# Order at the joints of an attention and clustering kernel: fillers dealt out anew, the last MLP sums by channel half, a fifth value pair ahead of the first score

## The chip, the cores and the metric

The kernel runs on one core of one Trainium2 chip. All data is float32. The metric is the device time in microseconds of one execution; the time before is the median of three.

TensorE multiplies matrices and writes to PSUM. VectorE (DVE in the profile), ScalarE (ACT) and GpSimd (POOL) do the rest, each through its own queue in the order in which the program issues its instructions. SyncE (SP) starts most transfers.

## The reference

The input x is 4 images of 256 channels by 64 x 64 positions. Two layers follow each other; N is 4096 positions of an image.

```python
# layer 0: attention over all positions
q = einsum('oc,bcn->bno', wq, xf) + bq          # 32 channels
k = einsum('oc,bcn->bon', wk, xf) + bk
attn = softmax(einsum('bnd,bdm->bnm', q, k), axis=-1)
v = einsum('oc,bcn->bon', wv, xf) + bv          # 256 channels
x = gamma * einsum('bcn,bmn->bcm', v, attn) + x
# layer 1: clustering, MLP, pointwise convolution
y = x + ls1 * cluster(group_norm(x, gn1_w, gn1_b), ...)
hdn = conv1x1(gelu(conv1x1(group_norm(y, gn2_w, gn2_b), w1)), w2)
y = y + ls2 * hdn
z = relu(batch_norm(y * dw_w))
z = relu(batch_norm(conv1x1(z, pw_w)))
```

`group_norm` takes one mean and one variance over a whole image. `cluster` makes features and values (96 channels each, 4 heads), cuts the image into 2 x 2 folds, pools 4 centres in each, gives every point to the centre that is most alike, sums the values of each centre's points, divides by their count, hands the result back to the points and projects it to 256 channels.

## The kernel before, in words

The images go through one after the other. In each there are three stages: attention, clustering, MLP. The order of all instructions is written by hand (`tc.manual_schedule()`), and so is the work of the next image that is slipped into the gaps of this one.

**Attention.** The positions are cut in 8 blocks of 512 queries, and 8 groups of 512 keys, so there are 64 units. `score` multiplies the keys of a group with the queries of a block (sc, L333), four 32-row products side by side. `exps` subtracts the column maximum, which has been spread over the partitions (mb, L383), and takes the exponential. `weigh` multiplies with the values (av, L408). Scores run ahead of the weighting by some units. For image 0 there is nothing to hide the beginning behind, and `alone` does it: keys (kp, L262), four blocks of queries (qp, L304), copies of the queries by DMA (q), value pairs (`v_pair`, two halves vp, L285, with one ScalarE copy, L293), and then the first 8 scores with a value pair behind each. Their maxima are folded (`fold`, L363), transposed (tt, L369) and reduced (L371), made a diagonal (dg, L373) and spread by a product (mb).

**Clustering.** `cluster` is a chain of many short steps on VectorE, ScalarE and TensorE. To keep TensorE busy in it there are *fillers*: a list of closures, from which each call `fill(n)` takes the next n. In images 0, 1 and 2 it is the list `projections` of the next image, 35 items:

```python
parts.projections = [lambda i=i: v_half(i) for i in range(N // P)]
parts.projections[26:26] = [lambda: k_half(0), lambda: q_four(0), lambda: k_half(1)]
```

so items 0 to 25 are value halves, 26 to 28 are the two key halves and the queries, and 29 to 34 the last six value halves. In image 3 the list comes from `late_block`: the last block of image 2's MLP, 16 matmuls `first`, 16 `second` (mol, L1005), an empty item and 4 `last` (pwl, L1028). The n of all calls add up to 35; what is left when the MLP begins is done there at once (`fill(N)`).

At the clustering's end stand, in the order of the program: a first sum over pooling weights (agg, L820), `similar(1)` and, after it, `fill(3)`; `largest(1)` and `weights(1)` on VectorE (to L760 and L763); the counts (cnt, L841), which need L760; the second sum; transposes; the projected centres gp with `fill(1)` behind; and then the hand-back in two rounds of four quarters and two channel halves (op, L911):

```python
products(0, 0, range(4))
products(0, 1, (0, 1))
seen(0, 0)
fill(2)
products(0, 1, (2, 3))
fill(2)
products(1, 0, range(4))
...
fill(5)
```

Channel half 0 is added to x by VectorE (L923), half 1 by ScalarE (L935) and GpSimd (L936). `seen` takes the statistics for the second group norm (`bn_stats`, L895). `group_norm` aggregates them (L214), averages over the partitions with two tiny matmuls (gnm, L216 and L217), has a filler, a third tiny matmul (gnv, L226), the root on ScalarE, and again fillers; then it loads the Gelu table, and the scale and shift are ready (L234, L235).

**MLP.** GpSimd makes three sums of weights (L1059 to L1061). Then come 8 blocks of 512 positions (7 in image 2), 4 steps each. `first` makes two hidden tiles from seven half-size products (hp, hu, hq, L1126), with sums on VectorE (L1162), and Gelu on ScalarE (L1155). `second` is a generator of four matmuls (mo, L1133) that add two hidden tiles i to two channel halves c; it is taken piece by piece between the products of the next step. For the last step of the last block two pieces are taken before the next image's maxima are transposed and two after. `finish` adds the sums to y (L1206) and appends the relu (L1196) to the hooks; `last` is the pointwise convolution (pw, L1102), whose output is evicted by ScalarE (L1112) and stored.

Of the kernel before, what the change touches and what calls it, by code (L numbers as in the profile page):

```python
# [13 lines left out]
P = 128  # L14
B, C, H, W = 4, 256, 64, 64
N = H * W
KC = C // P
# [6 lines left out]
HID = 4 * C  # L24
# [4 lines left out]
RG, GRP = 4, N // NB  # L29
# [16 lines left out]
def attention_then_cluster_block(  # L46
# [17 lines left out]
    nc = tc.nc  # L64
# [19 lines left out]
    def loaded(name, ap, shape):  # L84
        t = const.tile(shape, F32, name=name)
        nc.sync.dma_start(out=t, in_=ap)
        return t
# [38 lines left out]
    w2_s = loaded("w2_s", w2.rearrange("(k p) m -> p k m", p=P), [P, HID // P, C])  # L126
    wpw_s = loaded("wpw_s", wpw.rearrange("(k p) m -> p k m", p=P), [P, KC, C])
# [15 lines left out]
    def par(name, k=None):  # L143
        i = PC.index(name)
        return pc_s[:, :, i] if k is None else pc_s[:, k, i : i + 1]

    def pvc(name, p=P, off=0):
        i = PV[name] + off
        return pv_s[:p, i : i + 1]

    def rsqrt(dst, src, eps, meanwhile=lambda: None):

        nc.vector.tensor_scalar(dst, src, eps, None, ALU.add)
        nc.scalar.activation(dst, dst, AF.Sqrt)
        meanwhile()
        nc.vector.reciprocal(dst, dst)
# [49 lines left out]
    def table(f):  # L206

        nc.scalar.activation(probe, probe, f)

    def group_norm(b, which, stats, fill, meanwhile=lambda: None):  # L210

        nm = f"{which}_{b}"
        mv = small.tile([P, 2], F32, tag="mv", name=f"mv_{nm}")
        nc.vector.bn_aggr(mv, stats.rearrange("p i s -> p (i s)"))  # L214
        ps1 = ps_a.tile([P, NB], F32, tag="a0", name=f"gnm_{nm}")
        nc.tensor.matmul(ps1[:, 0:1], left, mv[:, 0:1], start=True, stop=True)  # L216
        nc.tensor.matmul(ps1[:, 1:2], avg, mv[:, 0:1], start=True, stop=True)  # L217
        fill(1)
        dv = small.tile([P, 2], F32, tag="dv", name=f"dv_{nm}")
        nc.vector.tensor_copy(dv, ps1[:, 0:2])  # L220
        nc.vector.scalar_tensor_tensor(
            mv[:, 1:2], dv[:, 0:1], dv[:, 0:1], mv[:, 1:2], ALU.mult, ALU.add
        )
        nc.vector.tensor_scalar(dv[:, 1:2], dv[:, 1:2], -1.0, None, ALU.mult)
        ps2 = ps_a.tile([P, NB], F32, tag="a1", name=f"gnv_{nm}")
        nc.tensor.matmul(ps2[:, 0:1], avg, mv[:, 1:2], start=True, stop=True)  # L226
        rstd = small.tile([P, 1], F32, tag="rstd", name=f"rstd_{nm}")
        rsqrt(rstd, ps2[:, 0:1], GN_EPS, meanwhile)
        fill(3 if which == "gn1" else 1)
        if which == "gn2":  # L230
            table(AF.Gelu_apprx_tanh)
        ga = small.tile([P, KC], F32, tag="ga", name=f"ga_{nm}")
        gb = small.tile([P, KC], F32, tag="gb", name=f"gb_{nm}")
        nc.vector.tensor_scalar(ga, par(f"{which}_w"), rstd, None, ALU.mult)  # L234
        nc.vector.scalar_tensor_tensor(gb, ga, dv[:, 1:2], par(f"{which}_b"), ALU.mult, ALU.add)  # L235
        return ga, gb
# [9 lines left out]
    def attention(b, xs):  # L246
# [7 lines left out]
        def k_half(i):  # L254

            if i == 0:
                own["k"] = big.tile([P, GRP, P], F32, tag="k", name=f"k_{b}")
            ps = ps_m.tile([P, 2, 2, P], F32, tag="m", name=f"kp_{b}_{i}")
            for t in range(2):
                for k in range(KC):  # L260
                    for r in range(RG):
                        nc.tensor.matmul(  # L262
                            ps[r * D : (r + 1) * D, t],
                            wqk_s[:, k, 1],
                            xs[2 * i + t][:, k].rearrange("p (g r n) -> p r g n", g=2, r=RG)[:, r],
                            start=(k == 0),
                            stop=(k == KC - 1),
                        )
            nc.scalar.activation(
                own["k"][:, 4 * i : 4 * i + 4, :].rearrange("p (t g) n -> p t g n", t=2),  # L270
                ps,
                AF.Identity,
                bias=bqk_s[:, 1:2],
            )
# [3 lines left out]
        def v_half(i):  # L278
            if i == 0:
                own["v"] = big.tile([P, N // P, C], F32, tag="v", name=f"v_{b}")  # L280
            if i % 2 == 0:
                vps[0] = ps_m.tile([P, 2, C], F32, tag="m", name=f"vp_{b}_{i // 2}")
            o = (i * P) % XT
            for k in range(KC):
                nc.tensor.matmul(  # L285
                    vps[0][:, i % 2, :],
                    xs[i * P // XT][:, k, o : o + P],
                    wv_s[:, k, :],
                    start=(k == 0),
                    stop=(k == KC - 1),  # L290
                )
            if i % 2:
                nc.scalar.copy(own["v"][:, i - 1 : i + 1, :], vps[0])  # L293

        def v_pair(i):
            v_half(2 * i)
            v_half(2 * i + 1)
# [165 lines left out]
        def alone():  # L463

            nc.vector.tensor_scalar(fb_w, ones[:ED], pvc("f_b", ED), None, ALU.mult)
            k_half(0)
            q_four(0)
            q_block(0, nc.gpsimd)
            q_block(1, nc.gpsimd)
            for i in range(4):  # L470
                v_pair(i)
            for u in range(GRP):
                if u == RG - 1:
                    k_half(1)
                hooks, maxima = [], []
                score(u, hooks, maxima)
                for f in hooks + maxima:
                    f()
                v_pair(u + 4)
            fold(0)  # L480
            for i in range(GRP + 4, GRP + 6):
                v_pair(i)
            half["dg"] = across(0)
            v_pair(GRP + 6)
            spread(0, half["dg"])
            v_pair(GRP + 7)
            exps(0)
            score(GRP)
# [133 lines left out]
    def cluster(b, ys, stats, cells, rest, fill, gelu):  # L622
# [30 lines left out]
        for k in range(KC):  # L653
# [4 lines left out]
                start=(k == 0),  # L658
                stop=(k == KC - 1),
# [118 lines left out]
        for nb in range(NBLK):  # L778
# [7 lines left out]
            ps = ps_s.tile([P, 2, 2, C], F32, tag="s", name=f"fv_{b}_{nb}")  # L786
            for j in range(4):
                g = j // 2
                for k in range(KC):
# [4 lines left out]
                        start=(k == 0),  # L794
                        stop=(k == KC - 1),
# [34 lines left out]
        heads(NBLK - 1)  # L830
        similar(1, lambda: fill(2))
        gelu(1)
        fill(3)
        table(AF.Sqrt)
        largest(1)
        weights(1)
# [3 lines left out]
        for j in range(8):  # L840
# [4 lines left out]
                start=(j == 0),  # L845
                stop=(j == 7),
# [9 lines left out]
        def turned(hb):  # L856
# [27 lines left out]
            start=True,  # L884
            stop=True,
# [64 lines left out]
        seen(0, 1)  # L950
        seen(1, 0)
        seen(1, 1)
        fill(5)
        return stats2


# [94 lines left out]
    def mlp(b, ys, stats2, fill, nxt, blocks):  # L1051
# [42 lines left out]
        def quarters(t):  # L1094
            return t[:, 0, :HB], t[:, 0, HB:], t[:, 1, :HB], t[:, 1, HB:]

        def last(nb):
            zs = pairs.pop(nb)
            ps = ps_s.tile([P, 2, NB], F32, tag="s", name=f"pw_{b}_{nb}")
            for c in range(KC):  # L1100
                for k in range(KC):
                    nc.tensor.matmul(  # L1102
                        ps[:, c, :],
                        wpw_s[:, k, c * P : (c + 1) * P],
                        zs[:, 1, k, :],
                        start=(k == 0),
                        stop=(k == KC - 1),
                    )

            def out_c(c):  # L1110
                o_s = zs[:, 0, c, :]
                nc.scalar.activation(  # L1112
                    o_s, ps[:, c, :], AF.Relu, scale=pw_s[:, c : c + 1], bias=pw_e[:, c : c + 1]
                )
                nc.sync.dma_start(out=ob[:, c, nb * NB : (nb + 1) * NB], in_=o_s)

            for c in range(KC):
                hooks.append(lambda c=c: out_c(c))
# [8 lines left out]

        def second(nb, acc, hs, j):

            for i in range(2):  # L1130
                jj = j + HID // P // 2 * i
                for c in range(KC):
                    yield nc.tensor.matmul(  # L1133
                        acc[c],
                        w2_s[:, jj, c * P : (c + 1) * P],
                        hs[:, i],
                        start=(j == 0 and i == 0),
                        stop=(j == HID // P // 2 - 1 and i == 1),
                    )

        def first(nb, j, todo):

# [71 lines left out]
        def hook():  # L1214
            while hooks:
                hooks.pop(0)()
# [5 lines left out]
        acc, todo = None, iter(())  # L1222
# [5 lines left out]
        for nb in range(blocks):  # L1228
            for j in range(4):
                hs = first(nb, j, todo)  # L1230
                if j == 0:
                    if nb:
                        finish(nb - 1, acc)
                    acc = [
                        ps_a.tile([P, NB], F32, tag=f"a{c}", name=f"mo{c}_{b}_{nb}")
                        for c in range(KC)
                    ]
# [20 lines left out]
        hook()  # L1258
        if nxt:
            nxt.exps(0)  # L1260
        last(blocks - 1)
        hook()
        if blocks < NBLK:
            y = []
# [14 lines left out]
    with tc.manual_schedule():  # L1279
# [3 lines left out]
        for b in range(B):  # L1283
# [10 lines left out]
            fill = filler(todo)  # L1294
# [81 lines left out]
```

## Time and profile before

| | |
|---|---|
| device time, median of 3 | 3477.98 us (3476.77 to 3483.36) |
| profiled span | 3476.0 us |
| TensorE busy | 3421.1 us (98%) |
| VectorE busy | 2046.2 us (59%) |
| ScalarE busy | 1683.9 us (48%) |
| GpSimd busy | 1489.2 us (43%) |
| mean granted TensorE clock | 0.997 of full |

A profile line of the timeline has a start in us from the span's start, a length in us, the engine, the line, the operation, what it writes and reads, the shape and how many instructions were merged; a bracket at the end tells how long the engine was idle before it, and which instruction ended that. Matmuls are pipelined, so the length of a merged line overlaps the next line's start a little, and it is the starts that show the pace. A float32 matmul counts as two instructions.

Image 0 takes from 0 to about 920 us, of which the attention ends at about 590, the clustering at about 670. The later images are laid out in the same way.

### The profile page before, as it was taken

Reading aid. Unit: us, or ns where it says so; the run is one execution under the profiler, and the core shown is the slowest. Engines: PE = TensorE matmul, PEld = TensorE weight load, DVE = VectorE, ACT = ScalarE, POOL = GpSimd, SP = SyncE. Lnnn points to the kernel's source line nnn. Section 1 sums busy time; section 2 is a strip of 40 time slices with the busy share of each in tenths; the row PEclk is TensorE's granted clock in tenths of the full one; section 3 lists DMA queues with packets and bytes.
Section 4 is the critical chain, followed back from the end, with each engine's and each line's share of the span. In section 5 each row is a group of like instructions: output and inputs, shape, how many; then the busy total and the mean of one; then the engine's idle time right before and its main releaser. Section 6 shows DMA issues by size and latency. Waiting matters only on the chain.

```text
span 3476.0 us, 31760 instructions
## 1 busy us (share of the span) xinstructions
PE 3421.1 (98%) x11760; PEld 1694.3 (49%) x11760; DVE 2046.2 (59%) x2912; ACT 1683.9 (48%) x2157; POOL 1489.2 (43%) x799
## 2 busy tenths in 40 slices
PE   8999999999999999999999999999999999999999
PEld 4444445655444444565544444466554444445565
DVE  4666664645566666464556666646446666664543
ACT  5545553444554554344455555434445554544444
POOL 2656665211265665521126566552104665672200
PEclk9999999999999999999999999999999999999999
DMA  2000001000000000100000000000000000000000
GB/s 91 7 4 3 7 0 49 7 19 13 20 5 4 3 7 12 37 7 19 19 16 4 3 5 5 19 30 7 19 19 10 4 7 3 4 0 1 13 19 25
DMA packets 25260, 47.16 MB, mean 14 GB/s; under 512 B 6704, under 2 KB 8592, under 8 KB 25104
## 3 DMA queue, kind: packets, MB, share of 16 engines
q1 hardware_dynamic: 20240, 38.29, 3.2%
q10 hardware_dynamic: 4608, 6.30, 0.8%
q8 instruction: 93, 1.52, 0.2%
q0 software_dynamic: 256, 0.52, 0.1%
q14 instruction: 63, 0.52, 0.0%
HBM read 19.93 MB, written 16.78 MB: 11 GB/s over the span
## 4 chain that ended last, share of the span: by engine, by line
PE 94%; DVE 3%; ACT 1%; DMA 0%; issue 0%; SPq 0%; POOL 0%; ACTq 0%; DVEq 0%
PE av L408 52%; PE mo L1133 12%; PE sc L333 8%; PE hu L1126 4%; PE pw L1102 3%; PE hp L1126 3%; PE hq L1126 3%; PE vp L285 2%; PE fv L790 2%; PE mb L383 1%; PE den L429 1%; PE op L911 1%; PE qp L304 0%; PE kp L262 0%; PE tt L369 0%
## 5 line engine op out<-in xcount | busy, mean ns | idle before, releaser
L408 PE MATMUL av<-s,v 128*128 128x512 f32 x4096 | 1826.5, 597 | 0.6 <-ACT s L398 0.6
L408 PEld LDWEIGHTS av<-s,v 128*128 128x128 f32 x4096 | 758.9, 190 | 1024.6 <-issue 1015.1
L403 POOL TENSOR_TENSOR acc<-acc,s 128x1024 f32<-128x1024 f32 x448 | 1057.5, 2361 | 466.1 <-ACT s L398 446.7
L398 ACT ACTIVATE s<-s 128x1024 f32<-128x1024 f32 x512 | 538.7, 1057 | 462.8 <-DVE s L395 429.4
L395 DVE TENSOR_TENSOR s<-s,mb 128x1024 f32<-128x1024 f32 x512 | 595.2, 1207 | 6.5 <-PE mb L383 6.5
L1133 PE MATMUL mo<-hs,w_s 128*128 128x512 f32 x992 | 508.4, 596 | 3.8 <-ACT hs L1155 1.6
L355 DVE TENSOR_TENSOR top<-sc,top 128x1024 f32<-128x1024 f32 x196 | 239.9, 1224 | 388.0 <-PE sc L333 388.0
L1155 ACT ACTIVATE hs<-hs,pv_s 128x256 f32<-128x256 f32 x496 | 251.3, 508 | 360.9 <-DVE hs L1162 350.1
L351 ACT COPY s<-sc 128x1024 f32<-128x1024 f32 x224 | 226.1, 1009 | 350.9 <-PE sc L333 350.9
L1162 DVE TENSOR_TENSOR hs<-hu,hs 128x256 f32<-128x256 f32 x372 | 157.8, 424 | 355.0 <-ACT hs L1165 205.5
L1088 POOL TENSOR_TENSOR xn<-xn 128x256 f32<-128x256 f32 x27 | 23.8, 881 | 681.7 <-DVE xn L1075 433.4
L333 PE MATMUL sc<-q,k 32*128 32x512 f32 x2048 | 294.0, 640 | 1.4 <-DMA q<-q 1.4
L400 POOL TENSOR_TENSOR acc<-s 128x1024 f32<-128x1024 f32 x32 | 75.1, 2347 | 476.9 <-ACT s L398 476.9
L358 DVE TENSOR_TENSOR top<-sc,top 128x1024 f32<-128x1024 f32 x196 | 240.1, 1225 | 47.5 <-ACT s L351 30.9
L356 ACT COPY s<-sc 128x1024 f32<-128x1024 f32 x224 | 226.9, 1013 | 76.0 <-DVE top L355 39.8
L1162 DVE TENSOR_TENSOR hs<-hq,hs 128x256 f32<-128x256 f32 x372 | 146.4, 421 | 107.5 <-PE hq L1126 103.3
L1133 PEld LDWEIGHTS mo<-hs,w_s 128*128 128x128 f32 x992 | 186.9, 190 | 42.7 <-ACT hs L1165 7.3
L333 PEld LDWEIGHTS sc<-q,k 32*128 32x128 f32 x2048 | 81.0, 182 | 192.5 <-issue 106.6
L1126 PE MATMUL hp<-xn,w_s 128*128 128x256 f32 x496 | 150.6, 385 | 2.7 <-DVE xn L1075 2.7
L1126 PEld LDWEIGHTS hp<-xn,w_s 128*128 128x128 f32 x496 | 92.4, 190 | 73.0 <-issue 62.4
L285 PE MATMUL vp<-wv_s,x 128*128 128x256 f32 x512 | 123.4, 387 | 0.2 <-ACT v L293 0.2
L1102 PE MATMUL pw<-xn,wpw_s 128*128 128x512 f32 x248 | 112.0, 594 | 3.4 <-ACT xn L1196 2.2
(215 smaller groups left out, 2823.0 us busy)
## 6 DMA issues: line engine op xcount, KB each, us to landing
x<-in_x SPq DMA_DIRECT2D x32, 512.0 KB, 4.6
out<-xn SPq DMA_DIRECT2D x62, 256.0 KB, 2.1
q<-q ACTq DMA_DIRECT2D x96, 64.0 KB, 2.0
w_s<-in_w SPq DMA_DIRECT2D x2, 1024.0 KB, 8.9
q<-q SPq DMA_DIRECT2D x24, 64.0 KB, 2.0
q<-q POOLq DMA_DIRECT2D x8, 64.0 KB, 6.4
out<-xl SPq DMA_DIRECT2D x2, 256.0 KB, 2.0
wv_s<-in_wv SPq DMA_DIRECT2D x1, 256.0 KB, 7.1
```

Of the source, the lines that this page charges most:

```text
L333: nc.tensor.matmul(halves[r // 2][:, r % 2, :], k_s[rows, g, :], q_s[rows, :], start=True, stop=True)
L355: nc.vector.tensor_tensor(top, halves[1], top, ALU.max)
L356: nc.scalar.copy(s[:, 2:4, :], halves[1])
L358: nc.vector.tensor_tensor(top, halves[0], top, ALU.max)
L395: nc.vector.tensor_tensor(sh, sh, mxs[nb].unsqueeze(1).to_broadcast([P, 2, NB]), ALU.subtract)
L398: nc.scalar.activation(sh, sh, AF.Exp)
L403: nc.gpsimd.tensor_tensor(acc, acc, s[:, 2 * h : 2 * h + 2], ALU.add)
L408: nc.tensor.matmul(av[c], own["v"][:, RG * g + quarter, c * P : (c + 1) * P], slots[u][:, quarter, :], start=(g == 0 and quarter == 0), st ...
L1126: nc.tensor.matmul(out, w[:, j * P : (j + 1) * P], x, start=True, stop=True)
L1133: yield nc.tensor.matmul(acc[c], w2_s[:, jj, c * P : (c + 1) * P], hs[:, i], start=(j == 0 and i == 0), stop=(j == HID // P // 2 - 1 and i ...
L1155: nc.scalar.activation(dst, src, act, bias=bias)
L1162: nc.vector.tensor_tensor(dst, ps, term, ALU.add)
```

## The change

It moves work and adds none. The fillers are dealt out anew: three more before the counts, four fewer after the last statistics, one more behind gnv in the second group norm. The sum stays 35, and the list's order is the same. It is meant to give TensorE something to do while VectorE works on `largest` and `weights`. The last four mo matmuls of an image's MLP are ordered by channel half, so that the first half's sum is complete after two of them, and the last pw product takes its inputs by k first, so that two of its four matmuls need only the first half's relu. And in image 0 a fifth value pair is put ahead of the first score, which waits for copies of the queries; the pairs behind the scores move up by one.

```diff
@@ group_norm
-        fill(3 if which == "gn1" else 1)
+        fill(3 if which == "gn1" else 2)
@@ alone
-            for i in range(4):
+            for i in range(5):
                 v_pair(i)
             for u in range(GRP):
...
-                v_pair(u + 4)
+                v_pair(u + 5)
             fold(0)
-            for i in range(GRP + 4, GRP + 6):
-                v_pair(i)
+            v_pair(GRP + 5)
             half["dg"] = across(0)
@@ cluster
         gelu(1)
-        fill(3)
+        fill(6)
         table(AF.Sqrt)
...
         seen(1, 1)
-        fill(5)
+        fill(1)
         return stats2
@@ mlp
-        def last(nb):
+        def last(nb, by_k=False):
...
-            for c in range(KC):
-                for k in range(KC):
-                    nc.tensor.matmul(
...
+            for c, k in ((0, 0), (1, 0), (0, 1), (1, 1)) if by_k else ((0, 0), (0, 1), (1, 0), (1, 1)):
+                nc.tensor.matmul(
...
         def second(nb, acc, hs, j):
-            for i in range(2):
+            order = [(i, c) for i in range(2) for c in range(KC)]
+            if nb == blocks - 1 and j == 3:
+                order.sort(key=lambda ic: ic[1])
+            for i, c in order:
                 jj = j + HID // P // 2 * i
...
-        last(blocks - 1)
+        last(blocks - 1, True)
         hook()
```

## The prediction

> **What bounds the kernel now.** I read four views: the page's busy times, TensorE's own waits, the timelines of the clustering's end in images 0 and 3, and the granted clock there. Page first:
>
> ```profile
> PE 3421.1 (98%) x11760; PEld 1694.3 (49%) x11760; DVE 2046.2 (59%) x2912; ACT 1683.9 (48%) x2157; POOL 1489.2 (43%) x799
> ```
>
> TensorE is the bound; no matmul is added or removed, so the time moves only by its idle time (55 us of 3476) and its clock. Its waits (us in total, times, longest) say where the edits can act:
>
> ```profile
> PE cnt L841 <- DVE scr L760: 9.9, 4, 2.7
> ...
> PE gnm_gn L216 <- DVE mv_gn L214: 3.9, 4, 3.2
> ...
> PE pw L1102 <- ACT xn L1196: 2.2, 4, 0.9
> ...
> PE sc L333 <- DMA q<-q: 1.4, 1, 1.4
> ```
>
> The cnt wait is what the three extra fillers are aimed at: 2.7 us in images 0 to 2, 1.7 in image 3. Now what follows it in image 0 (TensorE, then VectorE):
>
> ```profile
> 641.71 1.57 PE L841 MATMUL cnt<-scr,ones 128*96 128x64 f32 x16 [2.71 <-DVE scr L760]
> ...
> 649.27 1.99 PE L285 MATMUL vp<-wv_s,x 128*128 128x256 f32 x8
> ...
> 654.18 1.99 PE L911 MATMUL op<-simt,g 32*128 32x512 f32 x12
> 656.10 1.93 PE L262 MATMUL kp<-x,wqk_s 128*32 128x256 f32 x32
> 657.85 1.90 PE L304 MATMUL qp<-x,wqk_s 128*32 128x512 f32 x16
> ...
> 662.60 3.72 PE L285 MATMUL vp<-wv_s,x 128*128 128x256 f32 x16
> 666.15 0.28 PE L216 MATMUL gnm_gn<-mv_gn,left 128*128 128x1 f32 x2
> ```
>
> ```profile
> 655.36 2.73 DVE L923 SCALAR_TENSOR_TENSOR x<-op,pc_s,x 128x512 f32<-128x512 f32 x4 [1.72 <-PE op L911]
> 658.00 7.20 DVE L895 BATCH_NORM_STATS2 st<-x 128x6 f32<-128x512 f32 x12
> 665.24 0.59 DVE L214 BATCH_NORM_AGGREGATE mv_gn<-st 128x2 f32<-128x96 f32 x1
> ```
>
> From the second round of op (654.18) VectorE works without a pause to the statistics' end, and gnm, which opens the second group norm, comes 0.9 us after L214 began. TensorE has just enough fillers for it: gnm shows no wait. Image 3, whose fillers are shorter, shows the chain's bare length and what it is to lack fillers:
>
> ```profile
> 3213.76 1.99 PE L911 MATMUL op<-simt,g 32*128 32x512 f32 x12
> ...
> 3225.55 0.35 PE L216 MATMUL gnm_gn<-mv_gn,left 128*128 128x1 f32 x2 [3.20 <-DVE mv_gn L214]
> ```
>
> So op to gnm takes VectorE 11.79 us. Last the clock (after the stretch and its length: busy time of PE, PEld, DVE, ACT, POOL, then PEclk, DMA, GB/s):
>
> ```profile
> 3228.00:3229.00 1.00, 1.00 (x3) 0.60 (x3) 0.40 (x3) 0.20 (x1) 1.00 (x2) 0.50 0.00 0
> ...
> 1500.00:1508.00 8.00, 6.96 (x89) 6.41 (x89) 2.55 (x8) 1.02 (x4) 0.00 (x0) 0.57 0.00 0
> 2363.00:2368.00 5.00, 4.76 (x82) 4.50 (x83) 1.60 (x5) 0.04 (x1) 0.00 (x0) 0.66 0.02 3
> 641.00:646.00 5.00, 4.27 (x90) 3.82 (x91) 2.25 (x7) 0.90 (x4) 0.00 (x0) 1.00 0.00 0
> ```
>
> After the cnt wait of images 1 and 2, and the gnm wait of image 3, TensorE ran at half clock for a few us; after image 0's it did not. From cnt to the filler before op takes 4.69 us in image 0, 7.57 in image 1, 6.29 in image 2: half clock cost 2.9 and 1.6 us there.
>
> **What the Trainium skill says.** "TensorE: Matmul & The Clock Gate", What's actually happening: after an idle window of about 3.4 us, free-running, the array drops to half clock, and a busy window brings it back. The trace agrees (0.50 above), but 2.7 us of idle was enough twice in three times. "GPSIMD Engine Reference", Specifications: GpSimd shares SBUF interfaces with VectorE. The trace agrees: L221 takes 1.09 us while GpSimd makes the MLP's weight sums, and 0.22 in the first group norm, where GpSimd is idle. "TensorE: Matmul & The Clock Gate", Architectural detail: ScalarE's queue is strict first-in, first-out; so a table load waits behind a filler's copy (669.42, 0.59 us, then the load, 1.28 us).
>
> **The change part by part.**
>
> *Three fillers before cnt (images 0 to 2).* A half of a value pair takes 0.89 us (20 matmuls in 4.5), three take 2.67 and the wait was 2.71: cnt starts when it did and its idle time is gone. The half-clock spells after it go too; the trace has 4.5 us of them over three images. I take 1.7 us an image, since any phase of a free-running window can be met: of the ways in which a 2.7 us gap can fall on 3.4 us windows about three in four leave one window over half empty, at some 2.2 us each.
>
> *What is handed back.* The list of 35 fillers keeps its order, so all later calls get other items. The two calls between the first op and the second round of op held four value halves (2 times 1.93 us, 3.86). Now they hold a half, the first k half, q and the second k half: 0.93 + 1.8 + 1.83 + 1.8 = 6.36. VectorE had been idle there (1.72), so its chain starts 2.5 us later and gnm comes at 654.18 + 2.5 + 11.8 = 668.5, where it stood at 666.15: 2.3 later. Before gnm TensorE has op (1.92), two halves (1.93), op (1.06) and the lone filler (0.93), 5.84 us, against 11.79: **a new wait of 6.0 us at gnm**. Behind it on TensorE stand two more fillers and the whole MLP.
>
> *After gnm.* The shift of 2.3 shrinks: GpSimd's sums, over at 667.96 now, follow the last op, which comes 0.8 later, so they end by 668.8 and L221 costs 0.2 where it cost 1.09; TensorE's filler now ends last, and gnv comes 1.3 after gnm, where it took 1.88 (minus 0.6). Two fillers after gnv (1.8 us) fill the 0.91 wait of hp, but the Gelu table load stands behind the second one's copy and the first hidden copy 0.15 to 0.2 later than the rest. Net 1.9 to 2.1; I take 1.9.
>
> *Half clock after the new wait.* 6 us of idle fill a window in nearly every phase. The spell then lasts to the end of the first busy window, 3 to 6 us after gnm. Three value halves (2.7 us at full clock) and the MLP's first products lie in it; at spells of 3.4, 4.7 and 6.2 us I lose 1.6, 2.2 and 3.0. I take 2.1.
>
> Per image: 1.9 + 2.1 - 1.7 = +2.3 us; for three, **+7.0**.
>
> *Image 3.* Its fillers are the last block of image 2: 0.86 us matmuls. Three more cost 2.58 against a wait of 1.74, so cnt and all after it come 0.8 later. Matmul (7,0) moves ahead of the last op; its ScalarE relu waits for GpSimd and holds up op's evictions, some 0.3 more. The gnm wait grows from 3.2 to 6. Four pw matmuls follow gnv, where it was three, at half clock in part; the table load stands behind the first one's eviction. **+1.2** (0.3 to 2).
>
> *Fifth value pair before the first score.* Score 0 waits 1.41 us for the fourth q copy (landing at 26.2); a pair takes 1.78. Score 0 ends at 27.27 as now, one pair ahead. Seven pairs later one pair fewer stands between the last score and the transposes: TensorE gets there at 54.1, but fold ends at 54.9, so they start at 54.96 against 55.82. The 0.24 wait of the pair behind goes as well. **-1.1**.
>
> *MLP's last sums by half, pw by k.* In images 0 to 2 finish's first op stands behind dg on VectorE (ends 916.85; the sum was ready by 916.4), so it can't start earlier: 0. At the very end nothing stands before it: half 0's sum is ready 0.86 us sooner, its relu ends at 3465.85 where it was 3466.7, pw starts behind it and the k = 1 matmuls meet the second relu (3467.5) without a wait. The eviction waits for all four matmuls in both orders. **-0.8**.
>
> Sum: 7.0 + 1.2 - 1.1 - 0.8 = +6.3, and with the median of 3477.98 some **3484**.
>
> **The rivals.** (B) *The idle time is really gone*: gnm doesn't wait, the three cnt waits (8.1) and half-clock spells (4.5) are saved, less 0.8 in image 3, plus 1.9 at the ends: 13.7 at most, 3464 to 3470. For it: nothing is added. Against it: 11.79 us of chain and 5.84 us of fillers. (C) *Slower*: the half clock lasts a window longer (another 1.7 us an image) or the MLP's first products, which wait on VectorE five times there already, don't count as busy: 4 images more by 1 to 1.7, 3488 to 3491. For it: image 1's spell after cnt lasted two windows. Against it: image 2's and 3's lasted one.
>
> **How the numbers follow.** The forecast, 3480 to 3487, gets 0.62; C 0.28; B 0.10. The bound of 0.2% is 7 us, 3485: of the forecast 0.47 lies within, 0.15 above. So faster 0.10, within 0.47, slower 0.15 + 0.28 = 0.43. The range 3478.5 to 3490 holds the forecast and most of C and leaves B out.
>
> **What would show it.** Right: cnt without a wait in images 0 to 2; L262 and L304 between the two rounds of op; gnm waiting about 6 us in all four images, half clock after it and none after cnt; the first score's wait gone; pw's wait of 0.9 at the end gone and the three of 0.44 kept. Wrong, if gnm waits under 3 us, or if its L895 group starts at its old distance from cnt.

## The result and the profile after

The change makes the kernel slightly slower: 3489.02 us (median of 6 runs, 3486.53 to 3490.28) against 3479.43 for the kernel before in the same series. The ratio is 1.0027, with a 95% interval of 1.0014 to 1.0040. The profiled spans are 3486.0 and 3476.0 us, so the two traces hold a difference of 10 us as well. In the changed kernel the lines behind the edits have moved by one or two (cnt is L840, op L910, the MLP's products L1124); gnm keeps L216.

The page's busy times of after (engine, us, share of the span, instructions):

```profile
PE 3423.6 (98%) x11760; PEld 1696.6 (49%) x11760; DVE 2042.0 (59%) x2912; ACT 1683.2 (48%) x2157; POOL 1489.9 (43%) x799
```

With the same instructions TensorE is busy 2.5 us longer, at a mean granted clock of 0.994 where it was 0.997, and idle 62.4 us where it was 54.9. TensorE's waits of after (us in total, times, longest) name the idle time:

```profile
PE gnm_gn L216 <- DVE mv_gn L214: 24.0, 7, 6.0
...
PE hu L1124 <- DVE hs L1163: 7.6, 5, 3.8
...
PE pw L1100 <- ACT xn L1197: 1.4, 3, 0.5
...
PE tt L369 <- DVE top L363: 0.8, 1, 0.8
```

The 9.9 us of cnt have left the list, gnm has gone from 3.9 to 24.0, hu from 4.8 to 7.6. Pw keeps its three waits of under 0.5 and has lost the one of 0.9; the first score's 1.4 is now 0.2, and the transposes wait 0.8. TensorE's timeline of after at the end of image 0's clustering (start, length, shape; the bracket is the idle time before):

```profile
640.98 1.57 PE L840 MATMUL cnt<-scr,ones 128*96 128x64 f32 x16
...
646.63 1.99 PE L910 MATMUL op<-simt,g 32*128 32x512 f32 x12
648.55 1.13 PE L285 MATMUL vp<-wv_s,x 128*128 128x256 f32 x4
649.61 1.93 PE L262 MATMUL kp<-x,wqk_s 128*32 128x256 f32 x32
651.48 1.13 PE L910 MATMUL op<-simt,g 32*128 32x512 f32 x4
652.53 1.92 PE L304 MATMUL qp<-x,wqk_s 128*32 128x512 f32 x16
654.27 1.91 PE L262 MATMUL kp<-x,wqk_s 128*32 128x256 f32 x32
656.11 1.99 PE L910 MATMUL op<-simt,g 32*128 32x512 f32 x12
...
661.01 1.13 PE L285 MATMUL vp<-wv_s,x 128*128 128x256 f32 x4
667.90 0.56 PE L216 MATMUL gnm_gn<-mv_gn,left 128*128 128x1 f32 x2 [5.76 <-DVE mv_gn L214]
668.33 0.56 PE L217 MATMUL gnm_gn<-mv_gn,avg 128*128 128x1 f32 x2
668.75 2.05 PE L285 MATMUL vp<-wv_s,x 128*128 128x256 f32 x4
...
677.62 0.67 PE L1124 MATMUL hu<-xn,w_bac 128*128 128x256 f32 x2 [1.18 <-DVE hs L1163]
```

Cnt has no bracket any more. Both key halves and the queries stand between the two rounds of op, which are 9.48 us apart where they were 6.82. From the second round to gnm it is 11.79 us (667.90 - 656.11), and TensorE is idle for 5.76 of them. VectorE shows why:

```profile
657.29 2.73 DVE L922 SCALAR_TENSOR_TENSOR x<-op,pc_s,x 128x512 f32<-128x512 f32 x4 [4.38 <-PE op L910]
659.93 7.21 DVE L894 BATCH_NORM_STATS2 st<-x 128x6 f32<-128x512 f32 x12
667.17 0.59 DVE L214 BATCH_NORM_AGGREGATE mv_gn<-st 128x2 f32<-128x96 f32 x1
```

The chain is as long as before, and starts later: VectorE itself is idle 4.38 us ahead of it, where it was 1.72. The granted clock in windows of 2 us (busy time of PE, PEld, DVE, ACT, POOL; then PEclk), and one window behind cnt in image 1:

```profile
666.00:668.00 2.00, 0.10 (x1) 0.13 (x1) 1.72 (x3) 0.00 (x0) 2.00 (x2) 0.50 0.00 0
668.00:670.00 2.00, 2.00 (x7) 1.82 (x8) 0.44 (x3) 0.00 (x0) 0.21 (x1) 0.50 0.00 0
...
672.00:674.00 2.00, 2.00 (x6) 1.56 (x5) 1.87 (x5) 0.00 (x0) 0.00 (x0) 0.50 0.00 0
674.00:676.00 2.00, 1.71 (x7) 1.18 (x6) 0.96 (x3) 1.32 (x2) 0.00 (x0) 0.88 0.00 0
```

```profile
1504.00:1512.00 8.00, 7.86 (x111) 6.21 (x111) 3.11 (x9) 4.23 (x8) 0.00 (x0) 1.00 0.01 2
```

Half clock has moved from behind cnt to behind gnm. The difference of the two traces, measured between the same instructions (a joint is the way from the filler ahead of cnt to the first hu of w_bac):

| stretch | before | after | difference |
|---|---|---|---|
| start, to the first product that spreads the maxima (mb) | | | -0.7 |
| image 0, the joint | 38.60 | 43.93 | +5.33 |
| image 1, the joint | 41.48 | 43.40 | +1.92 |
| image 2, the joint | 40.21 | 43.12 | +2.91 |
| image 2's MLP, a wait of 3.8 at hu in both | | | -1.2 |
| image 3, the joint | 39.64 | 41.97 | +2.33 |
| last mo to last pw | 4.60 | 3.74 | -0.86 |
| last pw to the end | | | +0.3 |

That adds up to +10.0; the other stretches compared agree to 0.01 us.

### The profile page after: what moved, and what is told of

It is laid out like the page before. It is cut to its first block, busy times and chain, and to the rows that moved or that the text cites. A ratio compares the mean times of both kernels' runs of the same rounds, so it can differ in the third digit from the quotient of the medians.

```text
span 3486.0 us, 31757 instructions
## 1 busy us (share of the span) xinstructions
PE 3423.6 (98%) x11760; PEld 1696.6 (49%) x11760; DVE 2042.0 (59%) x2912; ACT 1683.2 (48%) x2157; POOL 1489.9 (43%) x799
## 4 chain that ended last, share of the span: by engine, by line
PE 94%; DVE 3%; ACT 1%; issue 0%; DMA 0%; POOL 0%; SPq 0%; ACTq 0%; DVEq 0%
PE av L408 52%; PE mo L1134 12%; PE sc L333 8%; PE hu L1124 4%; PE pw L1100 3%; PE hp L1124 3%; PE hq L1124 3%; PE fv L789 2%; PE vp L285 2%; PE mb L383 1%; PE den L429 1%; DVE st L894 1%; PE op L910 0%; PE qp L304 0%; PE tt L369 0%
## 5 line engine op out<-in xcount | busy, mean ns | idle before, releaser
L1124 PE MATMUL hp<-xn,w_s 128*128 128x256 f32 x496 | 150.4, 385 | 0.0
L1124 PEld LDWEIGHTS hp<-xn,w_s 128*128 128x128 f32 x496 | 92.8, 191 | 69.4 <-issue 62.4
```

Source lines behind the costliest of these rows:

```text
L1124: nc.tensor.matmul(out, w[:, j * P : (j + 1) * P], x, start=True, stop=True)
```

## The experiments

The theory: the fills handed TensorE's wait from cnt to gnm, by keeping VectorE's chain waiting for op, and the new wait costs half a clock as well. The rivals: the ends of the change (start, last sums) cost the time; or it is the clock alone; or the filler and the table load behind gnv. Each ratio is against the kernel before in the run's own series; the medians of before are 3479.43, 3479.64 and 3479.56 us, so after and the experiments can be compared across series to some tenths.

**Which part of the change.** e1 keeps the ends and puts the fills back, e2 is the kernel before with the fills alone.

```diff
e1, on after                                 e2, on before
-  fill(3 if which == "gn1" else 2)          -  fill(3 if which == "gn1" else 1)
+  fill(3 if which == "gn1" else 1)          +  fill(3 if which == "gn1" else 2)
-  fill(6)                                   -  fill(3)
+  fill(3)                                   +  fill(6)
-  fill(1)       # after seen(1, 1)          -  fill(5)       # after seen(1, 1)
+  fill(5)                                   +  fill(1)
```

> The changed kernel with the fillers dealt out as before: only the fifth value pair, the last sums by channel half and the last product by k are left. Theory (the fillers alone make the loss, the two ends gain 0.7 and 0.9 us): 1.6 us faster than before, some 3477.8. Rival (one of the ends costs, for instance the later transposes of image 0 or the k order): 2 us or more slower than before. Second rival (neither matters): within 0.5 us of before.

> The kernel before with the fillers dealt out anew and nothing else. Theory: the whole loss and 1.6 us more, 11 us slower than before, some 3490.5; gnm waits 5.8 us in images 0 to 2 and 6.0 in image 3. Rival (the loss comes from the ends, or from the sum of both): under 6 us slower.

e1 took 3478.22 us, ratio 0.9995 (0.9987 to 1.0003): by the time alone it can't be told from no change, though its median lies 1.4 us under before's, near the 1.6 expected, and its waits show the edits at work (pw 2.2 in four waits became 1.4 in three, the score's 1.4 is gone, the transposes wait 0.8). e2 took 3489.45, ratio 1.0029 (1.0018 to 1.0039): the whole loss, 9.8 us where 11 was expected, with gnm waiting 24.1 us in all. The ends are not to blame.

**Where the chain is held up.** e3 moves the keys and queries of the fillers' list back by three items, so that the two calls between the rounds of op take four value halves, as before, with all else as in after.

```diff
-    parts.projections[26:26] = [lambda: k_half(0), lambda: q_four(0), lambda: k_half(1)]
+    parts.projections[29:29] = [lambda: k_half(0), lambda: q_four(0), lambda: k_half(1)]
```

> The changed kernel with the two key halves and the queries three places later in the list of fillers, so that they fall behind the second round of op; the number of fillers in each call is as in the changed kernel. Theory (VectorE's chain starts late because long items stand between the two rounds of op): the second round of op starts 2.5 us earlier, gnm waits 3.4 us where it waited 5.8, the half-clock spells get shorter; the weight sums on GpSimd again meet L221, which gives 0.9 back: 5 to 8 us faster than the changed kernel, 3481 to 3484. Rival (only the number of fillers ahead of gnm matters): within 1.5 us of the changed kernel.

It took 3481.6 us, 1.0003 (0.9994 to 1.0011), so 7.4 us less than after. TensorE's timeline of e3:

```profile
646.19 1.99 PE L910 MATMUL op<-simt,g 32*128 32x512 f32 x12
...
653.01 1.99 PE L910 MATMUL op<-simt,g 32*128 32x512 f32 x12
...
665.51 0.56 PE L216 MATMUL gnm_gn<-mv_gn,left 128*128 128x1 f32 x2 [2.99 <-DVE mv_gn L214]
```

The rounds are 6.82 us apart again, and gnm still comes 12.5 us after the second (here a wait of 0.81 for the copy of the keys falls in between). The same 35 fillers with the long ones three places later halve the wait in images 0 to 2; image 3, whose list is another, keeps its 6.0. What counts is which filler stands where.

**The clock by itself.** e4 leaves after's order and puts six products into TensorE's gnm wait. They go to a scratch tile that nobody reads; they are work outside the reference's computation.

```diff
         fill(1)
+        idle = ps_m.tile([P, NB], F32, tag="m", name=f"warm_{b}")
+        for _ in range(6):
+            nc.tensor.matmul(idle, ones, w1_s[:, 0, :NB], start=True, stop=True)
         return stats2
```

> The changed kernel with six 128x512 products of constants into a scratch tile, which nothing reads, after the lone filler: 5.2 us of TensorE work inside the wait at gnm, outside the reference's computation. Theory (a good half of the loss is the half clock that follows the wait): the wait at gnm shrinks to under 1 us, the clock stays full, and the work after gnm runs 2 to 3 us faster in each of four images: 8 to 11 us faster than the changed kernel, 3478 to 3481. Rival (VectorE's chain sets the time and TensorE's clock is hidden behind it): within 1.5 us of the changed kernel.

```profile
662.60 5.31 PE L955 MATMUL warm<-w_s,ones 128*128 128x512 f32 x12
668.53 0.35 PE L216 MATMUL gnm_gn<-mv_gn,left 128*128 128x1 f32 x2 [0.62 <-DVE mv_gn L214]
...
675.03 0.67 PE L1127 MATMUL hu<-xn,w_bac 128*128 128x256 f32 x2 [0.30 <-DVE hs L1166]
```

e4 took 3479.12 us, 0.9998 (0.9990 to 1.0007): 9.9 us less than after, although useful work waits for the same VectorE chain. From gnm to hu it takes 6.50 us instead of 9.72. So half clock behind gnm, with what follows from it, cost about 10 us by the medians. In image 3 the profiled run, at 3482.22 us the slowest of the twelve, gained nothing: the wait at gnm fell to 0.91 us, but gnv, right behind, waits 1.37, half clock covers 6.83 us there, and the joint takes 42.51 where it took 41.97.

e6 does the same in the kernel before, ahead of cnt (three products, two in image 3, behind `fill(3)`).

```diff
         fill(3)
+        idle = ps_s.tile([P, 2, NB], F32, tag="s", name=f"warm_{b}")
+        for _ in range(3 if b + 1 < B else 2):
+            nc.tensor.matmul(idle[:, 0], ones, w1_s[:, 0, :NB], start=True, stop=True)
```

> The kernel before with three 128x512 products of constants into a scratch tile that nothing reads (two in image 3), after the three fillers that precede the counts: TensorE is busy in the wait of 2.7 us, outside the reference's computation, and no real work is moved. Theory (the wait at the counts costs by the half clock after it, since the idle time itself is VectorE's): no half clock after the counts, 3 to 5 us faster than before. Rival (the wait at the counts itself is what costs): no gain, within 1 us of before.

```profile
1500.00:1508.00 8.00, 7.84 (x101) 5.50 (x99) 3.96 (x11) 3.57 (x7) 0.00 (x0) 1.00 0.01 2
```

Where the kernel before had 0.57 the clock is full. The time is 3473.12 us, 0.9983 (0.9977 to 0.9990), 6.4 us under before, against 3 to 5 expected. The two profiled spans differ by 3.8 only (3476.0 and 3472.2). The granted clocks of all runs point to the rest. The kernel before spread over 10.6 us in 38 runs of this series, and its slower runs had the lower clock: the mean span is 3475.3 us at 0.997 (3 runs), 3476.1 at 0.996 (28), 3479.5 at 0.995 (6) and 3484.4 at 0.994 (1). The profiled run, at 0.997, had less half clock than most; the 20 runs of e6 had 0.997 to 0.999. Which waits the other runs paid for, no trace shows.

The two runs with scratch products tell apart what the new order costs by itself and what the clock adds. The joints of images 0, 1 and 2:

| | image 0 | image 1 | image 2 |
|---|---|---|---|
| before | 38.60 | 41.48 | 40.21 |
| e6: before's order, clock full | 38.6 | 38.6 | 38.6 |
| after | 43.93 | 43.40 | 43.12 |
| e4: after's order, clock full | 40.7 | 40.7 | 40.7 |

At full clock the new order is 2.1 us an image longer, 6.3 in all. Half clock took 4.5 us in before and takes 8.3 in after, 3.8 more. Together that is the 10.2 us of the three joints: the greater part of the loss is the later chain, the smaller part the clock. The medians of e4 and e6 differ by 6.0 us, which is in line, though their ends and image 3 differ as well.

**The table load.** In e8 the Gelu table is loaded ahead of the two fillers behind gnv.

```diff
-        fill(3 if which == "gn1" else 2)
         if which == "gn2":
             table(AF.Gelu_apprx_tanh)
+        fill(3 if which == "gn1" else 2)
```

> The changed kernel with the load of the Gelu table ahead of the two fillers behind gnv, where it stood behind them and so behind the second one's copy on ScalarE. Theory (the table load, held up by that copy, keeps the first hidden copy and with it the second hu product): the wait of 1.18 us there falls to about 0.3 in images 0 to 2, 2 to 3 us faster than the changed kernel. Rival (TensorE at half clock is the bound there): within 1 us of the changed kernel.

ScalarE's timeline of after first, then TensorE's of e8:

```profile
674.66 0.59 ACT L293 COPY v<-vp 128x512 f32<-128x512 f32 x1 [3.13 <-PE vp L285]
675.26 1.28 ACT L208 ACT_TABLE_LOAD   x1
676.56 0.20 ACT L208 ACTIVATE probe<-probe 128x1 f32<-128x1 f32 x1
676.66 0.35 ACT L1166 COPY hs<-hp 128x256 f32<-128x256 f32 x1
```

```profile
673.24 0.67 PE L1124 MATMUL hu<-xn,w_abcd 128*128 128x256 f32 x2 [0.47 <-ACT hs L1166]
673.75 0.59 PE L1124 MATMUL hq<-xn,w_s 128*128 128x256 f32 x2
674.59 0.67 PE L1124 MATMUL hu<-xn,w_bac 128*128 128x256 f32 x2 [0.25 <-DVE hs L1163]
```

In after the load waits for the copy of the second filler, whose products run at half clock, so that the copy starts at 674.66; the first hidden copy stands behind the load, and hu waits 1.18 us for the sum made from it. In e8 the load is long done and hu waits 0.25, 0.93 less, in each of images 0 to 2. The time, 3486.09 us, 1.0018 (1.0011 to 1.0025), is 2.9 lower than after's, about three times 0.93; the two intervals overlap, so it is the trace that carries this. Half clock doesn't fall alike in the two traces, but where it ends at like distances behind gnm (5.48 us in after and 5.63 in e8, 4.93 and 5.04) the way from gnm to hu is 0.85 and 0.88 us shorter in e8.

**Fillers that fit both chains.** e5 keeps the three fillers ahead of cnt, but leaves only two value halves between the rounds of op, and puts keys, queries and the rest beside the statistics.

```diff
-        fill(3 if which == "gn1" else 2)
+        fill(3 if which == "gn1" else 1)
-    parts.projections[26:26] = [lambda: k_half(0), lambda: q_four(0), lambda: k_half(1)]
+    parts.projections[28:28] = [lambda: k_half(0), lambda: q_four(0), lambda: k_half(1)]
         seen(0, 0)
-        fill(2)
+        fill(1)
         products(0, 1, (2, 3))
-        fill(2)
+        fill(1)
         products(1, 0, range(4))
...
         seen(1, 1)
-        fill(1)
+        fill(4)
```

> The changed kernel with the fillers dealt out once more: six before the counts as in the change, one instead of two in each of the two calls ahead of the second round of op, four after the last op, one after gnv, and the keys and queries two places later in the list. Theory (VectorE's chain from the second round of op sets the end, so short fillers ahead of it and long ones behind it pay): the second round of op starts 1.8 us earlier than in the kernel before, gnm waits under 1 us in images 0 to 2, no half clock there, 2 us plus the spell of 1.5 an image; with the ends 10 to 13 us faster than before, 3466 to 3470. Rival (the moved fillers run into buffers or copies that aren't free): within 3 us of before.

```profile
650.57 1.99 PE L910 MATMUL op<-simt,g 32*128 32x512 f32 x12
...
660.05 1.99 PE L285 MATMUL vp<-wv_s,x 128*128 128x256 f32 x8
662.27 0.38 PE L216 MATMUL gnm_gn<-mv_gn,left 128*128 128x1 f32 x2 [0.23 <-DVE mv_gn L214]
```

```profile
651.75 2.73 DVE L922 SCALAR_TENSOR_TENSOR x<-op,pc_s,x 128x512 f32<-128x512 f32 x4 [0.34 <-PE op L910]
```

3464.0 us, 0.9957 (0.9943 to 0.9970): 15.6 us under before, where 10 to 13 were expected. The second round of op comes 5.45 us behind the first (9.48 in after), VectorE waits only 0.34 us for it, and gnm finds its fillers just used up. This is what the change was for. Image 3, whose list differs, keeps a wait of 4.07; e7 fills that one with four scratch products, again outside the reference's computation (the edit is against e5).

```diff
         fill(4)
+        if b == B - 1:
+            idle = ps_s.tile([P, 2, NB], F32, tag="s", name=f"warm_{b}")
+            for _ in range(4):
+                nc.tensor.matmul(idle[:, 0], ones, w1_s[:, 0, :NB], start=True, stop=True)
```

> The run dealt out once more, with four such products ahead of gnm in image 3, whose fillers are too short for VectorE's chain. Theory: the half clock after that wait is gone, 1.5 to 3 us faster than without them. Rival: no difference.

The window behind gnm in image 3, of e5 and then of e7:

```profile
3212.00:3220.00 8.00, 7.52 (x16) 3.78 (x17) 4.43 (x13) 3.89 (x7) 3.34 (x3) 0.69 0.09 33
```

```profile
3212.00:3220.00 8.00, 6.22 (x20) 2.73 (x19) 6.28 (x15) 4.55 (x8) 4.97 (x4) 1.00 0.09 33
```

3461.47 us, 0.9949 (0.9937 to 0.9962), 2.5 below e5 by the medians of five runs each, and the fastest here. The two intervals overlap; in the traces the joint of image 3 is 1.74 us shorter (37.55 after 39.29).

## Why the prediction was right, and which terms were mis-sized

The mechanism held, and the time lies within the stated range of 3478.5 to 3490. It lies above the forecast's own 3480 to 3487, though, and in rival C's 3488 to 3491. Of the 5 us above 3484, 1.45 come from the time of before (3477.98 then, 3479.43 in the series of the comparison); the change cost 9.6 us where 6.3 were forecast. The loss of 0.27% is just past the bound of 0.2%; the prediction had given 0.47 to a time within it and 0.43 to a loss past it. Taken by the prediction's own steps:

- *Cnt.* Right: no wait in images 0 to 2. The half clock saved was taken as 1.7 us an image, 5.1; from the filler ahead of cnt to gnm it was 31.73, 34.61 and 33.34 us before and is 34.21 three times now, so the spells had cost 2.88 and 1.61, together 4.5, which is 0.6 less. As an average 1.7 was good: in e1, with the same waits at cnt, that way takes 33.32, 34.71 and 33.33, and over the six waits of the two traces the spells cost 1.8 each.
- *What is handed back.* Right in place and size: the second round came 2.66 us later within the two rounds (2.5 forecast), the chain took 11.79, gnm comes 2.48 later than in image 0 before (2.3), and waits 5.8 to 6.0 (6.0). It adds 0.5 over three images.
- *After gnm.* Right at full clock: in e4 it takes 6.50 us from gnm to hu where it was 6.87, the forecast's -0.4. In image 0 L221 takes 0.22 now, and gnv follows gnm by 2.70 at half clock (1.39 in e4, 1.3 forecast).
- *Half clock behind gnm* is the term that was mis-sized. From gnm to hu the three images take 9.72, 9.18 and 8.91, together 8.3 more than three times 6.50; forecast were 2.1 an image, 6.3. The forecast let the spell end 3 to 6 us behind gnm, and it ended 6.57, 5.48 and 4.93 us behind it. With windows of 3.41 us, the shortest spell in these traces, and read as the prediction reads them, the first window that is busy throughout ends 3.4 to 6.8 us behind gnm (an estimate), so the range was set too low; where in it an image falls is chance. The forecast's own prices (2.2 us at 4.7, 3.0 at 6.2), drawn on in a straight line, give about 8.1 for the three spells. That they fit is in part luck, because two errors cancel: the table load, taken as 0.15 to 0.2 an image beside them, makes 0.93, 2.8 in all (e8), which leaves 5.5 for half clock alone. The two are linked: half clock delays the filler, the filler its copy, the copy the load. Three small errors beside this one of 2.0 make the joints +10.2 instead of +7.0 (three times 2.3 is 6.9; the prediction rounds up).
- *Rival C* had the time right, but not the way to it. The spells of images 0 and 3 are a window longer than those of images 1 and 2 (10.24 against 6.83), but that window lies in the idle time: they begin 3.67 and 3.56 us ahead of gnm. Behind gnm none of the four lasts over 6.7 us.
- *Image 3.* +2.33 instead of +1.2. Gnm comes 0.84 later behind the filler, near the 0.8 and 0.3 forecast; then it takes 10.57 us to hu where it took 9.10, because half clock covers 6.68 us behind gnm, and before 3.41. The forecast left little for that.
- *Start.* -0.7 instead of -1.1: the fourth copy of the queries landed at 26.7 instead of 26.2, so the score still waits 0.17; the transposes then wait for fold, as forecast (0.79), and start 0.28 earlier than before (55.54 after 55.82), where 0.86 were forecast; the pair behind them, without its wait, gives the rest.
- *Last sums.* Right: the wait of 0.89 at the end is gone (-0.86), the others are kept. The output's end gives back 0.3.
- *Not foreseen:* -1.2 in image 2's MLP, where the same wait of 3.8 us was followed by 3.41 us of half clock instead of 6.83. No edit touches that wait; it was luck, and it hid part of the loss.

Rival B was wrong for this order and right as an aim: e5, with the waits of images 0 to 2 gone, takes 3464.0, at the lower end of B's 3464 to 3470.

## What to carry to other kernels

A filler has two sides: it hides the chain beside it, and it delays the chain that its own engine has yet to start. So put short fillers ahead of the product that releases the longest chain of another engine, and long ones beside that chain; the same 35 items gave 3489.0 and 3464.0 us. Where no useful filler is left, price a wait as its length plus the half clock behind it, with all that hangs on work slowed by it, and consider products into a scratch tile. Two orders are compared best with the clock kept full in both; here that parted 6.3 us of order from 3.8 us of half clock.

## What the runs showed of the hardware

- All stretches at half clock on record, in the traces of before, after and all eight experiments, were 3.41, 6.83 or 10.24 us long, multiples of 3.41, wherever the waits lay (the one that the program's end cuts off left out; the clock's record begins some 16 us into the program). The Trainium skill ("TensorE: Matmul & The Clock Gate", What's actually happening) speaks of free-running windows of about that length, and the traces agree. Which wait is punished, and for how many windows, is therefore partly chance: the 2.71 us at cnt of image 0 brought no half clock in before and 3.41 us of it in e1, and the same wait in image 1 brought 6.83 in both. Half clock followed waits of 2.70 to 2.71 us at cnt in five cases of six (before and e1), waits of 2.99 at gnm in three of three (e3), and waits of 5.76 to 6.04 in all thirteen (after, e2, e3, e8). How empty a window must be is not shown, and one stretch, in e6 at 27.47, stands behind no wait of over 0.17 us but behind the first score; its cause is open.
- Keeping TensorE busy with work that nobody reads was worth 9.9 us in after (24 products), 6.4 in before (11) and 2.5 in e5 (4), by the medians. It was not sure to work at each wait: see image 3 of e4.
- L221 on VectorE, with a 128x1 tile, took up to 1.26 us in before, while GpSimd's weight sums ran, and 0.22 in image 0 of after, where those sums had ended. The 64 statistics of 128x512 (L895) took 0.675 to 0.687 us each, those beside GpSimd's sums included.
